# One over the deviation as a power on GpSimd, and a convolution's first products behind four PSUM copies

## Chip, cores, metric

One core of one Trainium2 chip. The metric is the device time of one execution in microseconds. All arithmetic is fp32. A program on one core shows no second die to compare with, so single runs are marked "unknown" in state; executions of the kernel before fall in two groups, near 3418 us and from 3435 to 3448 us.

## The reference, cut to what matters

A shifted-window transformer block on x of shape (16, 192, 56, 56), then a depthwise 3x3 convolution whose taps are computed from the mean of its input.

```
def _ln(x, g, b, eps=1e-05):
    mu = x.mean(-1, keepdims=True)
    var = ((x - mu) ** 2).mean(-1, keepdims=True)
    return (x - mu) / jnp.sqrt(var + eps) * g + b
# block: x1 = x + proj(attention(_ln(x)));  x2 = x1 + fc2(gelu(fc1(_ln(x1))))
# convolution: taps = f(mean(x2)), mask leaves 4 of 9 taps, one filter a channel
```

Each layer norm needs 1/sqrt(var + eps) for every pixel. The means are folded into the weights, so this factor is all that a norm applies.

## The kernel before

The 56 rows of an image are worked in four rounds, each on a strip of 7 rows in both halves. The first two rounds have no MLP (the two products fc1 and fc2) and two at the end have no attention; a short start and tail surround them. The statistics come from matmuls with a constant 1/192, already spread over groups of 32 partitions. `norm_devs` turns them into factors, for norm 1 of a later strip and norm 2 of an earlier one at once:

```
def norm_devs(keys):
    ...
    for s in sides:
        nc.scalar.activation(d[var[s]], stats[s][mean[s], :T], AF.Square)
    for s in sides:
        nc.vector.tensor_tensor(d[var[s]], stats[s][var[s], :T], d[var[s]], ALU.subtract)
    p = slice(0, 128) if len(sides) == 2 else var[sides[0]]
    nc.scalar.activation(d[p], d[p], AF.Sqrt, bias=eps_t[p])
    table(AF.Gelu)                        # a dummy that loads the table
    nc.vector.reciprocal(d[p], d[p])      # T = 392 columns
```

The main loop, with cuts:

```
for i in range(2, NS + 2):
    dev = norm_devs(keys)
    norm1_scale(i + 1, ...)               # VectorE
    norm_spread(keys, dev)                # 16 DMAs
    mlp_first(i - 2, ..., between)        # between: one convolution piece
    table(AF.Exp)
    attention_scores(i, ...)              # ends in 4 products "prob" on GpSimd
    table(AF.Sqrt)
    ys = [(*c, conv_begin(*c)) for c in conv_ready(2)]   # y = x * tap + bias, ScalarE
    mlp_out(i - 2, *mlp_second(i - 2, hid, turn))        # turn: PE transposes prob, ScalarE copies it
    yns[i - 1] = norm2_scale(...)         # GpSimd, needs the spread factors
    norm_squares(...)                     # GpSimd
    o = attention_values(i, prts)
    for c in ys: conv_rest(*c)            # 3 taps a piece, VectorE
    qs[i + 1] = attention_qk(i + 1)       # VectorE: kbd <- pk
    tail_of(i, o)                         # projection, then v
```

Each engine works its instructions in this order. `attention_turn` uses two PSUM buffers in turn, so the third turn needs the copy of the first.

Names of tiles in the profiles: `st` are the statistics, `dev` the factors and `dv` the factors spread over the partitions, `yn` and `win` the inputs scaled by them, `sq` the squares for the next statistics. `pk`, `pq`, `pe` and `pv` are the products for q, k and v in PSUM, `kbd` the keys copied out of it. `sc` are the scores, `e` their exponentials, `tot` one over their sum, `prob` the probabilities, `pt` the turned ones in PSUM and `prt` their copy. `po` and `o` are the values, `pp` the projection, `ph` and `pf` the two MLP products with `hid` between them. `y` is a piece of the convolution.

Of the kernel before, what the change touches and what calls it, by code (L numbers as in the profile page):

```python
# [8 lines left out]
F32 = mybir.dt.float32  # L9
AF = mybir.ActivationFunctionType  # L10
ALU = mybir.AluOpType
# [9 lines left out]
T = WS * IMG  # L21
# [8 lines left out]
EPS = 1e-5  # L30
# [6 lines left out]
def tile_swin_then_dynamic_conv(  # L37
# [31 lines left out]
    nc = tc.nc  # L69
# [4 lines left out]
    const = ctx.enter_context(tc.tile_pool(name="const", bufs=1))  # L74
# [7 lines left out]
    def bank(name, k):  # L82
        return psum.tile([128, 512], F32, tag=f"bank{k}", name=name)

    def banks(name, k):
        return psum.tile([128, 2, 512], F32, tag=f"banks{k}", name=name)

    def mm(dst, lhs, rhs, start, stop):
        nc.tensor.matmul(dst, lhs, rhs, start=start, stop=stop, skip_group_check=True)  # L89
# [81 lines left out]

    ident = const.tile([128, 128], F32, tag="ident", name="ident")
    eps_t = const.tile([128, 1], F32, tag="eps", name="eps_t")
    junk = const.tile([1, 1], F32, tag="junk", name="junk")

    sel = const.tile([128, 3, 32], F32, tag="sel", name="sel")
# [43 lines left out]
    def flat_of(i):  # L220
        v0, v1 = rows_of(i)
        return v0.rearrange("p h r c -> p h (r c)"), v1.rearrange("p r c -> p (r c)")

    sqs, stats = {}, {}

    def table(func):

        nc.scalar.activation(junk, eps_t[0:1], func)  # L228
# [28 lines left out]
    def norm_devs(keys):  # L257


        sides = sorted(keys)  # L260
        d = one.tile([128, T], F32, tag="dev", name=f"dev_{keys[sides[0]]}")
        mean = {s: slice(s * 64, s * 64 + 64) for s in sides}
        var = {s: slice(64 - s * 64, 128 - s * 64) for s in sides}
        for s in sides:
            nc.scalar.activation(d[var[s]], stats[s][mean[s], :T], AF.Square)
        for s in sides:
            nc.vector.tensor_tensor(d[var[s]], stats[s][var[s], :T], d[var[s]], ALU.subtract)
        p = slice(0, 128) if len(sides) == 2 else var[sides[0]]
        nc.scalar.activation(d[p], d[p], AF.Sqrt, bias=eps_t[p])  # L269
        table(AF.Gelu)  # L270
        nc.vector.reciprocal(d[p], d[p])  # L271
        stats.clear()
        return d

# [13 lines left out]
    def norm1_scale(i, dv, engine):  # L288

        v0, v1 = rows_of(i)  # L290
        b4 = dv.rearrange("p h (r c) -> p h r c", c=IMG)
        w0 = win0[:, :, :, 0:N].rearrange("p h w (r c) -> p h r w c", c=WS)
        w1_ = win1[:, :, 0:N].rearrange("p w (r c) -> p r w c", c=WS)
        cut = WS - SHIFT
        for ws, cs, at, n in (
            (slice(0, NWIN - 1), slice(0, WS), SHIFT, NWIN - 1),
            (slice(NWIN - 1, NWIN), slice(0, cut), IMG - cut, 1),
            (slice(NWIN - 1, NWIN), slice(cut, WS), 0, 1),
        ):
            m = n * (cs.stop - cs.start)  # L300

            def wide(v):
                return v[..., at : at + m]

            for h in range(2):
                engine.tensor_tensor(
                    w0[:, h, :, ws, cs],
                    wide(v0[:, h]).rearrange("p r (w c) -> p r w c", w=n),
                    wide(b4[:, h]).rearrange("p r (w c) -> p r w c", w=n),
                    ALU.mult,  # L310
                )
            for h in range(2):
                p = slice(h * 64, h * 64 + 64)
                engine.tensor_tensor(
                    w1_[p, :, ws, cs],
                    wide(v1[p]).rearrange("p r (w c) -> p r w c", w=n),
                    wide(b4[p, h]).rearrange("p r (w c) -> p r w c", w=n),
                    ALU.mult,
                )
# [268 lines left out]
    def mlp_second(i, hid, turn):  # L588
        pf1, pf = bank(f"pf1_{i}", 0), banks(f"pf_{i}", 2)
        for f in range(NFC):  # L590
            for a in range(2):
                mm(
                    pf1[a * 64 : a * 64 + 64, :T],
                    wf2[:, f, C0:DIM],
                    hid[:, f, a],
                    f == 0,
                    f == NFC - 1,
                )
        for f in range(NFC):
            for a in range(2):  # L600
                mm(pf[:, a, :T], wf2[:, f, 0:C0], hid[:, f, a], f == 0, f == NFC - 1)
            if f >= 2:
                turn(f - 2)
        return pf1, pf
# [3 lines left out]
    def mlp_out(i, pf1, pf):  # L608

        b, s = divmod(i, STEPS)  # L610
        if s == 0:
            sums[b] = small.tile([128, 2, STEPS], F32, tag="sums", name=f"sums_{b}")
        v0, v1 = flat_of(i)
        nc.vector.scalar_tensor_tensor(
            v1, pf1[:, :T], f2b[1], v1, ALU.add, ALU.add, accum_out=sums[b][:, 1, s : s + 1]
        )
        nc.vector.scalar_tensor_tensor(  # L617
            v0, pf[:, :, :T], f2b[0], v0, ALU.add, ALU.add, accum_out=sums[b][:, 0, s : s + 1]
        )
# [35 lines left out]
    def conv_begin(b, wt, n):  # L655

        kc, lo = (0, n * PR) if n < 4 else (1, (n - 4) * PR)
        y = work.tile([128, PR, IMG], F32, tag="y", name=f"y_{b}_{n}", bufs=3)
        nc.scalar.activation(  # L659
            y,  # L660
            images[b][kc][:, lo : lo + PR],
            AF.Identity,
            bias=cb[kc],
            scale=wt[:, kc, 1:2],
        )
        return y
# [36 lines left out]
    def has(i):  # L703
        return 0 <= i < NS

    def conv_ready(k):

        ready = []
        while k and convs and "wt" in convs[0]:
            c = convs[0]  # L710
            ready.append((c["b"], c["wt"], c["n"]))
            c["n"] += 1
            k -= 1
            if c["n"] == 6:
                convs.pop(0)
        return ready

    def stats_of(i):
        keys = {}
        if has(i + 2):  # L720
            keys[0] = f"1_{i + 2}"
            norm_stats(keys[0], i + 2, 0)
        if has(i - 1):
            keys[1] = f"2_{i - 1}"
            norm_stats(keys[1], i - 1, 1)
        return keys
# [9 lines left out]

    make_identity(nc, ident)
    nc.vector.memset(eps_t, EPS)
    nc.vector.memset(sel, 0.0)
    nc.vector.memset(sel[:, 0], 1.0 / DIM)  # L740
    nc.vector.memset(sel[0:64, 1], 1.0 / DIM)
# [49 lines left out]
    for c, at, lo, n, be, bias in (  # L791
# [5 lines left out]
        p = slice(at, at + n)  # L797
# [4 lines left out]
    for t in [kbd, vbd] + prob:  # L802
        nc.gpsimd.memset(t, 0.0)
    keys = stats_of(-1)
    dev = norm_devs(keys)
    norm1_scale(0, dvs.pop(0), nc.vector)
    dvs.update(norm_spread(keys, dev))
# [5 lines left out]
    for h in range(2):  # L813
        p = slice(h * 64, h * 64 + 64)
# [108 lines left out]
    for i in range(2, NS + 2):  # L923
        keys = stats_of(i)
        dev = norm_devs(keys) if keys else None
        if has(i + 1):
            norm1_scale(i + 1, dvs.pop(0), nc.vector)
        if keys:
            dvs.update(norm_spread(keys, dev))
        if (i + 3) % STEPS == 0 and (i + 3) // STEPS < B:  # L930
            b = (i + 3) // STEPS
            images[b] = load_x(b, nc.sync)

        def between():
            for b, wt, n in conv_ready(1):
                conv_rest(b, wt, n, conv_begin(b, wt, n))
            if convs and "pooled" in convs[-1]:
                convs[-1]["wt"] = taps(convs[-1]["b"], convs[-1].pop("pooled"))

        hid = one.tile([128, NFC, 2, T], F32, tag="hid", name=f"hid_{i - 2}")  # L940
        mlp_first(i - 2, yns.pop(i - 2), hid, between)
        if has(i):
            table(AF.Exp)
            attention_scores(i, *qs.pop(i))
        table(AF.Sqrt)
        ys = [(*c, conv_begin(*c)) for c in conv_ready(2)]
        prts = []

        def turn(wp):
            if has(i):  # L950
                prts.append(attention_turn(i, wp))

        mlp_out(i - 2, *mlp_second(i - 2, hid, turn))
        if 1 in keys:
            yns[i - 1] = norm2_scale(i - 1, dvs.pop(1))
        if has(i + 3):
            norm_squares(f"1_{i + 3}", i + 3, 0, nc.gpsimd)
        o = attention_values(i, prts) if has(i) else None
        for c in ys:
            conv_rest(*c)  # L960
        if has(i + 1):
            qs[i + 1] = attention_qk(i + 1)
        tail_of(i, o)
        if (i - 2) % STEPS == STEPS - 1:
            b = (i - 2) // STEPS
            convs.append({"b": b, "n": 0, "pooled": taps_pool(b)})
    c = convs.pop()
# [77 lines left out]
```

## Time and profile before

| | before |
|---|---|
| time, us | 3435.07 (3417.78 to 3435.66, 3 runs) |
| profiled span, us (an execution of 3416.78) | 3415.0 |
| TensorE busy | 95% |
| GpSimd busy | 22% |
| table loads on ScalarE | 193 of 1283 ns |
| wait of the transposes for ScalarE's copy | 86.4 us |
| reciprocal over 392 columns, VectorE | 2.60 us |

TensorE has no pause in a round but the one in front of the third turn. The lines are in the prediction. The starts of the first MLP product in the chain that ended last give the length of a round: 50.15, 50.14, 52.45 and 52.01 us in one image, the longer two being those with two convolution pieces behind the turns.

### The profile page before, as it was taken

How to read it: one execution, taken by the hardware profiler on the slowest of the kernel's cores; microseconds unless marked ns; L12 is line 12 of the kernel's file. 1: busy time of each engine (PE TensorE's matmuls, PEld its weight loads, DVE VectorE, ACT ScalarE, POOL GpSimd, SP SyncE). 2: the span in 40 equal slices, each digit the busy share in tenths (PEclk: the TensorE clock that was granted, in tenths of full speed). 3: DMA queues.
4: the chain of work that ended last, by engine and by line, in shares of the span. 5: the costliest groups of instructions: out<-in, count | busy, mean ns of one | idle time of the engine just before them, and what ended most of it. 6: DMA issues, size and time to landing. Idle time of an engine off the chain costs nothing.

```text
span 3415.0 us, 65067 instructions
## 1 busy us (share of the span) xinstructions
PE 3241.5 (95%) x26642; PEld 1917.0 (56%) x26642; DVE 2256.0 (66%) x4143; ACT 1755.0 (51%) x2863; POOL 745.6 (22%) x656
## 2 busy tenths in 40 slices
PE   4799999999999999999999999999999999999996
PEld 2455555555555555555555555555555555555553
DVE  5455676767667576676767667576676767667563
ACT  2355555555555555555555555555555555555552
POOL 4221221221221221221221221221221221221210
PEclk8799999999999999999999999999999999999998
DMA  3100111111011111111111011111111111011001
GB/s 94 19 20 23 46 39 48 34 53 34 25 48 44 43 34 40 42 39 48 34 53 34 25 48 46 41 34 39 44 39 48 34 53 34 25 48 46 12 29 44
DMA packets 79125, 135.40 MB, mean 40 GB/s; under 512 B 21766, under 2 KB 61692, under 8 KB 76908
## 3 DMA queue, kind: packets, MB, share of 16 engines
q1 hardware_dynamic: 77266, 128.54, 13.1%
q8 instruction: 210, 3.44, 0.4%
q0 software_dynamic: 1056, 1.92, 0.3%
q10 hardware_dynamic: 506, 0.79, 0.1%
q14 instruction: 87, 0.71, 0.1%
HBM read 41.25 MB, written 38.54 MB: 23 GB/s over the span
## 4 chain that ended last, share of the span: by engine, by line
PE 68%; DVE 20%; ACT 7%; issue 3%; DMA 1%; POOL 0%; SPq 0%; DVEq 0%; ACTq 0%; POOLq 0%
PE ph L89 24%; PE pv L89 7%; PE pp L89 7%; DVE top L459 6%; DVE e L453 5%; PE po L89 5%; PE st L89 5%; DVE e L460 5%; PE pk L89 4%; PE pq L89 4%; PE pe L89 4%; PE pf L89 3%; DVE tot L467 3%; PE pt L500 3%; ACT L228 2%
## 5 line engine op out<-in xcount | busy, mean ns | idle before, releaser
L469 POOL TENSOR_TENSOR prob<-e,tot 113x588 f32<-113x588 f32 x256 | 297.7, 1174 | 2483.4 <-PE pf L89 2177.1
L89 PE MATMUL ph<-yn,wf 128*128 128x392 f32 (+1 forms) x3072 | 818.6, 508 | 1.1 <-ACT hid L572 1.1
L89 PE MATMUL pf<-hid,wf 128*64 128x392 f32 (+1 forms) x3072 | 819.5, 498 | 0.0
L89 PEld LDWEIGHTS ph<-yn,wf 128*128 128x128 f32 (+1 forms) x3072 | 410.0, 188 | 401.2 <-ACT hid L572 84.8
L89 PEld LDWEIGHTS pf<-hid,wf 128*64 128x64 f32 (+1 forms) x3072 | 377.1, 164 | 310.8 <-issue 121.6
L572 ACT ACTIVATE hid<-ph,f1b 128x784 f32<-128x784 f32 x384 | 336.8, 913 | 243.2 <-PE ph L89 242.8
L360 DVE TENSOR_SCALAR kbd<-pk,qkb 32x784 f32<-32x784 f32 x256 | 263.8, 1030 | 254.8 <-PE pk L89 251.6
L463 ACT ACTIVATE e<-e 113x588 f32<-113x588 f32 x256 | 177.3, 693 | 466.5 <-DVE e L460 466.4
L674 DVE SCALAR_TENSOR_TENSOR y<-x,wt,y 128x770 f32<-128x770 f32 x288 | 322.9, 1131 | 22.7 <-ACT y L659 15.9
L453 DVE TENSOR_TENSOR e<-sc,bias_t 113x588 f32<-113x588 f32 x256 | 188.5, 737 | 190.0 <-PE sc L89 189.7
L500 PE MATMUL pt<-ident,prob 113*128 113x113 f32 x1536 | 195.3, 264 | 86.4 <-ACT prt L506 86.4
L89 PE MATMUL pv<-wqkv,win 64*128 64x192 f32 (+1 forms) x2048 | 273.1, 328 | 3.1 <-DVE kbd L360 3.1
L500 PEld LDWEIGHTS pt<-ident,prob 113*128 113x128 f32 x1536 | 168.7, 142 | 187.4 <-issue 131.2
L423 DVE COPY vbd<-pv 49x192 f32<-49x192 f32 x512 | 159.6, 350 | 172.2 <-PE pv L89 86.8
L89 PEld LDWEIGHTS pv<-wqkv,win 64*128 64x128 f32 (+1 forms) x2048 | 251.8, 188 | 35.3 <-issue 18.1
L89 PE MATMUL pp<-o,wp 128*128 128x392 f32 (+2 forms) x896 | 251.5, 521 | 1.6 <-ACT o L532 1.6
L228 ACT ACT_TABLE_LOAD x193 | 247.6, 1283 | 3.5
L617 DVE SCALAR_TENSOR_TENSOR x<-pf,cols,x 128x784 f32<-128x784 f32 x64 | 66.2, 1035 | 246.5 <-PE pf L89 246.5
L506 ACT COPY prt<-pt 128x678 f32<-128x678 f32 x256 | 176.9, 714 | 98.5 <-PE pt L500 98.5
L425 ACT COPY vbd<-pv 49x192 f32<-49x192 f32 x512 | 135.3, 312 | 151.8 <-DVE vbd L423 145.4
L271 DVE RECIPROCAL dev<-dev 128x392 f32<-128x392 f32 (+1 forms) x67 | 174.4, 2602 | 48.7 <-ACT dev L269 48.7
L460 DVE TENSOR_TENSOR e<-e,top 113x588 f32<-113x588 f32 x256 | 199.4, 779 | 8.7
(139 smaller groups left out, 4119.5 us busy)
## 6 DMA issues: line engine op xcount, KB each, us to landing
dv<-dev SPq DMA_DIRECT2D x1020, 49.0 KB
x<-in_x_dram SPq DMA_DIRECT2D x15, 1484.0 KB
out_dram<-y SPq DMA_DIRECT2D x48, 392.0 KB
out_dram<-y SPq DMA_DIRECT2D x48, 196.0 KB
x<-in_x_dram SPq DMA_DIRECT2D x16, 392.0 KB
x<-in_x_dram SPq DMA_DIRECT2D x15, 350.0 KB
out_dram<-y SPq DMA_DIRECT2D x16, 308.0 KB
out_dram<-y SPq DMA_DIRECT2D x16, 154.0 KB
```

The source lines that it names most:

```text
L89: nc.tensor.matmul(dst, lhs, rhs, start=start, stop=stop, skip_group_check=True)
L228: nc.scalar.activation(junk, eps_t[0:1], func)
L360: nc.vector.tensor_scalar(kbd[p, 0:2, :, h % 2, :], pk[p, :, :T].rearrange("p h (w t) -> p h w t", t=N), qkb[p, 1:2], None, ALU.add,)
L453: nc.vector.tensor_tensor(e, sc[:PW, :, : HEADS * N], rel, ALU.add)
L459: nc.vector.tensor_reduce(t, ehs[wp], AX.X, ALU.max)
L460: nc.vector.tensor_tensor(ehs[wp], ehs[wp], t.broadcast_to([PW, 2 * HEADS, N]), ALU.subtract)
L463: nc.scalar.activation(es[wp], es[wp], AF.Exp)
L469: nc.gpsimd.tensor_tensor(prob[wp][:PW, :, 0:N], ehs[wp], t.broadcast_to([PW, 2 * HEADS, N]), ALU.mult)
L500: nc.tensor.transpose(pt[:, a, g * PW : (g + 1) * PW], prob[wp][:PW, h : h + 2, :].rearrange("p h k -> p (h k)"), ident[:PW, :PW],)
L506: nc.scalar.copy(prt, pt[:, :, : 3 * PW])
L572: nc.scalar.activation(hid[:, f], phs[f][:, :, :T], AF.Gelu, bias=f1b[:, f : f + 1])
L674: nc.vector.scalar_tensor_tensor(dst, src, wt[:, kc, t : t + 1], dst, ALU.mult, ALU.add)
```

## The change

The intent is to take the root's table from ScalarE (three loads a round become two) and 2.6 us of reciprocal from VectorE, by putting one power on GpSimd, which is idle for over 30 us a round. The first products of the convolution then move behind the copies, so that nothing stands between the exponentials and the copies.

```diff
+    power = const.tile([128, 1], F32, tag="power", name="power")
...
-            nc.vector.tensor_tensor(d[var[s]], stats[s][var[s], :T], d[var[s]], ALU.subtract)
+            nc.vector.scalar_tensor_tensor(
+                d[var[s]], stats[s][var[s], :T], EPS, d[var[s]], ALU.add, ALU.subtract
+            )
         p = slice(0, 128) if len(sides) == 2 else var[sides[0]]
-        nc.scalar.activation(d[p], d[p], AF.Sqrt, bias=eps_t[p])
-        table(AF.Gelu)
-        nc.vector.reciprocal(d[p], d[p])
+        n = p.stop - p.start
+        nc.gpsimd.tensor_tensor(d[p], d[p], power[p].broadcast_to([n, T]), ALU.pow)
...
+    nc.vector.memset(power, -0.5)
...
-        table(AF.Sqrt)
-        ys = [(*c, conv_begin(*c)) for c in conv_ready(2)]
         prts = []
...
         mlp_out(i - 2, *mlp_second(i - 2, hid, turn))
+        table(AF.Gelu)
+        ys = [(*c, conv_begin(*c)) for c in conv_ready(2)]
```

## The prediction

> **What bounds the kernel now.** I read the page's first part, then the table of waits, then the timeline of one round of the main loop, engine by engine. One round handles one strip of seven rows in each image half: statistics, first MLP product, attention scores, second MLP product with the four transposes ("turns") of the probabilities between its steps, values, q/k, projection, v. There are 64 full rounds.
>
> ```profile
> PE 3241.5 (95%) x26642; PEld 1917.0 (56%) x26642; DVE 2256.0 (66%) x4143; ACT 1755.0 (51%) x2863; POOL 745.6 (22%) x656
> ```
>
> TensorE is busy 95% of 3415 us. It idles for only 174 us, and some 90 us of that lie in the start and the tail. So no change that leaves its products alone can win much over 2.5%. The table of waits names the one idle time that recurs every round:
>
> ```profile
> PE pt L500 <- ACT prt L506: 86.4, 64, 5.7
> ```
>
> That is 86.4 us in 64 waits, all in front of a transpose that waits for ScalarE to copy an earlier one out of PSUM (two buffers alternate, so the third turn needs the first one's copy). The timeline of a round with convolution work, and of one without, shows why the copy is late:
>
> ```profile
> 1064.66 0.69 ACT L463 ACTIVATE e<-e 113x588 f32<-113x588 f32 x1 [2.48 <-DVE e L460]
> 1065.37 1.28 ACT L228 ACT_TABLE_LOAD   x1
> 1066.66 0.20 ACT L228 ACTIVATE junk<-eps_t 1x1 f32<-1x1 f32 x1
> 1066.77 1.96 ACT L659 ACTIVATE y<-x,cols,wt 128x784 f32<-128x784 f32 x2
> 1068.64 1.31 ACT L506 COPY prt<-pt 128x678 f32<-128x678 f32 x2
> ...
> 1069.48 0.77 PE L500 MATMUL pt<-ident,prob 113*128 113x113 f32 x6 [2.22 <-ACT prt L506]
> ```
>
> ```profile
> 965.01 0.77 PE L500 MATMUL pt<-ident,prob 113*128 113x113 f32 x6 [0.35 <-ACT prt L506]
> ```
>
> Between the last exponential and the first copy stand the load of the root's table (1.4 us until the next instruction) and, in convolution rounds, two first products (1.96 us). TensorE then stands for 2.22 us, or for 0.35 us in the other rounds. My count of rounds: 15 images have their convolution behind a later image's rounds, each with two rounds that hold two such products, so 30 convolution rounds x 2.22 = 66.6 us. The other 32 ordinary rounds x 0.35 = 11.2 us. The first two rounds give the rest (2.56 and 5.66 us in their timeline). The sum is 86.0, against 86.4 in the table.
>
> VectorE's side of the same convolution round:
>
> ```profile
> 1071.62 1.03 DVE L617 SCALAR_TENSOR_TENSOR x<-pf,cols,x 128x784 f32<-128x784 f32 x1 [4.69 <-PE pf L89]
> 1072.58 0.08 DVE L617 DVE_READ_ACCUMULATOR x<-pf,cols,x 128x1 f32 x1
> 1072.58 3.22 DVE L674 SCALAR_TENSOR_TENSOR y<-x,wt,y 128x770 f32<-128x770 f32 x2
> 1075.83 0.19 DVE L683 COPY y<-cols 128x56 f32<-128x56 f32 x1
> 1076.06 4.06 DVE L674 SCALAR_TENSOR_TENSOR y<-x,wt,y 128x770 f32<-128x770 f32 x4
> 1080.16 4.17 DVE L360 TENSOR_SCALAR kbd<-pk,qkb 32x784 f32<-32x784 f32 x4
> ...
> 1085.10 1.14 PE L89 MATMUL pv<-wqkv,win 64*128 64x192 f32 x12
> ```
>
> From the MLP's addition to the end of the kbd eviction (1084.33) VectorE has no pause. The v product (pv) takes over the PSUM banks that kbd is read from, so it can't start before 1084.33. It starts at 1085.10, when TensorE gets there. **The slack is only 0.77 us.** This decides my prediction.
>
> **What the Trainium skill says.** "ScalarE: Activation LUTs", section "What ACT_TABLE_LOAD costs": about 1283 ns for the load plus about 1380 ns of drain. The trace agrees with the first (193 loads, 1283 ns each), but not with the second here: the next instruction starts 0.01 us after the load ends. So I count 1.4 us a load, not 2.66. "VectorE: DVE Perf Modes", section "First, the fixed hardware budget", has the reciprocal as an iterative divide with a repeat count of 8. The trace has 2.60 us for 392 columns, 6.4 cycles each at that page's 0.96 GHz. "GPSIMD Engine Reference", section 3.1, has no figure for a power. It gives some 2.6 cycles an element at 1.2 GHz for a two-input product and about three operations a cycle for longer bodies. The trace's 392-column square takes 0.84 us alone (1.56 us beside VectorE's convolution), which is 2.6 cycles. Section 8 of that page says that GpSimd contends with VectorE instructions with two SBUF inputs. The trace agrees: the two convolution taps that run beside GpSimd's last products take 1.61 us each, the next four 1.02 us.
>
> **The change, part by part.**
>
> Root and reciprocal go. ScalarE loses a root (0.62 us) and one of three table loads each round, VectorE 2.60 us. Both stand at the head of the round, behind which ScalarE waits for TensorE (0.83 us before the first GELU) and VectorE too (1.84 us before the first scores, 5.27 us without convolution). So these 2.6 us by themselves only lengthen waits and win nothing. What counts is that the load no longer precedes the copies.
>
> The power comes. The variance is ready at 1042.2 in this round and GpSimd is idle until 1059.4:
>
> ```profile
> 1059.40 1.17 POOL L469 TENSOR_TENSOR prob<-e,tot 113x588 f32<-113x588 f32 x1 [36.44 <-PE pf L89]
> ```
>
> So up to 17 us are free. The first turn starts at 1063.27 with its input done at 1060.57, so some 20 us cost little. Behind it, 16 DMAs spread the result, issued over 11.2 us with the half that this round uses first. GpSimd uses that at 1068, which leaves a power of up to some 16 us room too. If a power is 60 operations (my assumption) at the page's three a cycle, 392 columns take 6.5 us, an estimate. I take 8. That is free.
>
> The first products move behind the copies. The copies can then start at 1065.35, after the last exponential. The first is done at 1066.0, before TensorE reaches the third turn at 1067.26, and that turn's input from GpSimd is done at 1066.9. So the gap closes in every round. In ordinary rounds nothing else binds (VectorE waits 7.50 us for pk there): 32 x 0.35 = 11 us.
>
> In convolution rounds TensorE comes 2.2 us sooner, but VectorE doesn't. The fourth copy ends at about 1070.7. Then come the GELU load with its dummy (1.4) and the first product (1.03), so the first y is ready at 1073.15, against 1072.58 when VectorE begins its taps today. The taps and kbd take the same 11.75 us and end at 1084.9, and pv can start at 1084.95 rather than 1085.10: a gain of 0.15 us, not 2.2. In the other convolution round of an image, kbd waits 0.27 us for pk today, so the same sum gives 0.4 us. 15 x 0.15 + 15 x 0.4 = 8 us.
>
> The start: in the first two rounds the root and its loads precede the copies by 2.56 and 5.66 us of TensorE's idle time. I count 6 of these 8 us. The first scaling on VectorE no longer stands behind a reciprocal: 3 us. The tail has one GELU load less in front of a product: 1 us.
>
> The sum: 11 + 8 + 6 + 3 + 1 = 29 us, which makes 3417 into 3388. Two of the three runs of before took 3435, so a median may fall in either group. I take 3395.
>
> **The rivals.** (1) VectorE doesn't hold the convolution rounds, because the taps run faster when GpSimd's products lie beside the exponentials' end and not beside them. Then all 86 us come back: about 3330. Against it: six taps at 1.02 us still make 6.1 instead of 7.3 us, which frees 1.2 us a round at most, 30 x 1.2 = 36 us more, so about 3352; GpSimd's own times hardly move, so I expect little of that. (2) The power takes over 20 us. Then each us more holds up the probabilities, the turns and TensorE, 64 us for each us: a 30 us power makes about 4050. For it: no row here shows a power. Against it: 61 cycles a column are free, 23 times a product. (3) The ScalarE copies of the values (o) come behind load and products, to about 1075.0 in place of 1075.03, while TensorE is 2.2 us sooner and needs their bank for pe at about 1075.6. That is 0.5 us of slack; if it fails, convolution rounds may lose instead of gain: about 3405 to 3415.
>
> **Range and chances.** The sum gives about 1% and its parts are each bounded by a gap that I measured, so the middle is narrow: 3368 to 3425, the upper end for no gain in the slower group. Faster by over 2% needs over 68 of the 86 us, and so rival 1 in full: 8%. Slower by over 2% is rival 2: 12%. Within 2%: 80%.
>
> **What would show it.** The wait of pt for prt falls from 86.4 us to under 5. Table loads fall from 193 to some 130. Ordinary rounds fall from 50.15 to about 49.8 us. Convolution rounds stay above 51.4 us, with a new wait of pv for VectorE's kbd of some 2 us, 30 times, and a new wait of VectorE's taps for y. The power shows as a GpSimd row of 67 instructions under 17 us, and prob waits for tot as before. I am wrong if the power's row is over 20 us, or if convolution rounds fall to 50 us with no new wait.

## The result

The changed kernel takes **6433.6 us** (6432.49 to 6434.05, 4 runs), against 3426.68 us (4 runs) of the kernel before. The ratio is 1.877 (1.871 to 1.884). Ratios here are the mean time of one kernel's fast runs over that of the other's of the same rounds, so not quite the ratio of the medians.

The first part and the costliest groups of the page of the changed kernel (columns: line, engine, operation, tiles, shapes, count, then busy us and mean ns of one, then idle time before):

```profile
PE 3392.6 (53%) x26642; PEld 2003.7 (31%) x26642; DVE 2089.0 (32%) x4077; ACT 1614.2 (25%) x2654; POOL 4943.9 (77%) x723
...
L273 POOL TENSOR_TENSOR dev<-dev,power 128x392 f32<-128x392 f32 (+1 forms) x67 | 4223.2, 63033 | 1115.4 <-DVE dev L268 1092.1
```

GpSimd, at 22% before, is at 77%. One power takes 63.0 us, and there are 67. The table of waits of the changed kernel:

```profile
PE pt L502 <- POOL prob L471: 2667.9, 62, 43.6
```

No wait of the transposes for ScalarE's copy stands near the top any more. In its place they wait 43 us in each of 62 rounds for the probabilities. The timeline of GpSimd over one round shows the queue:

```profile
2012.06 63.05 POOL L273 TENSOR_TENSOR dev<-dev,power 128x392 f32<-128x392 f32 x1 [20.24 <-DVE dev L268]
2075.08 4.57 POOL L471 TENSOR_TENSOR prob<-e,tot 113x588 f32<-113x588 f32 x4
2082.56 1.84 POOL L327 TENSOR_TENSOR yn<-x,dv 128x784 f32<-128x784 f32 x1 [2.91 <-issue]
2084.36 2.10 POOL L330 TENSOR_TENSOR yn<-x,dv 64x392 f32<-64x392 f32 x2
2086.54 1.49 POOL L240 TENSOR_TENSOR sq<-x 128x784 f32<-128x784 f32 x1
2087.99 0.84 POOL L241 TENSOR_TENSOR sq<-x 128x392 f32<-128x392 f32 x1
2108.50 63.05 POOL L273 TENSOR_TENSOR dev<-dev,power 128x392 f32<-128x392 f32 x1 [19.66 <-DVE dev L268]
```

The four products that make the probabilities had their inputs by 2036.2. They run only when the power is done, at 2075, all four together. What follows is serial: turns, values, q/k, projection, statistics, and then the next variance, 33 us after the first product. A round lasts 63.05 + 33 = 96 us. Four power starts in a row lie 96.16, 94.94, 95.25 and 96.12 us apart.

TensorE also works more slowly just after such a pause. In this round its granted clock was 0.50 from 2076 to 2080 us, 0.90 to 2084 and 1.00 from 2085, and the first turn took 1.39 us where it takes 0.74 us in the kernel before. This is a small part: in all, TensorE's busy time grew from 3241.5 to 3392.6 us, by 151 of the 3007 us lost.

### The profile page after: what moved, and what is told of

The parts are those of the page before. It is cut to its first block, busy times and chain, and to the rows that moved or that the text cites. A ratio compares the mean times of both kernels' runs of the same rounds, so it can differ in the third digit from the quotient of the medians.

```text
span 6432.2 us, 65166 instructions
## 1 busy us (share of the span) xinstructions
PE 3392.6 (53%) x26642; PEld 2003.7 (31%) x26642; DVE 2089.0 (32%) x4077; ACT 1614.2 (25%) x2654; POOL 4943.9 (77%) x723
## 5 line engine op out<-in xcount | busy, mean ns | idle before, releaser
L273 POOL TENSOR_TENSOR dev<-dev,power 128x392 f32<-128x392 f32 (+1 forms) x67 | 4223.2, 63033 | 1115.4 <-DVE dev L268 1092.1
L502 PE MATMUL pt<-ident,prob 113*128 113x113 f32 x1536 | 254.5, 316 | 2668.4 <-POOL prob L471 2667.9
L502 PEld LDWEIGHTS pt<-ident,prob 113*128 113x128 f32 x1536 | 220.9, 177 | 2796.1 <-POOL prob L471 2706.8
L89 PE MATMUL pf<-hid,wf 128*64 128x392 f32 (+1 forms) x3072 | 904.1, 528 | 0.0
L89 PEld LDWEIGHTS pf<-hid,wf 128*64 128x64 f32 (+1 forms) x3072 | 413.4, 176 | 333.6 <-issue 162.2
L676 DVE SCALAR_TENSOR_TENSOR y<-x,wt,y 128x770 f32<-128x770 f32 x288 | 291.2, 1021 | 181.9 <-ACT y L661 175.1
L89 PE MATMUL st<-sq,sel 128*32 128x392 f32 x1024 | 189.0, 512 | 118.8 <-POOL sq L240 118.1
L327 POOL TENSOR_TENSOR yn<-x,dv 128x784 f32<-128x784 f32 x64 | 118.4, 1851 | 147.0 <-DMA dv<-dev 91.8
```

What stands on the lines that cost most here:

```text
L89: nc.tensor.matmul(dst, lhs, rhs, start=start, stop=stop, skip_group_check=True)
L273: nc.gpsimd.tensor_tensor(d[p], d[p], power[p].broadcast_to([n, T]), ALU.pow)
L502: nc.tensor.transpose(pt[:, a, g * PW : (g + 1) * PW], prob[wp][:PW, h : h + 2, :].rearrange("p h k -> p (h k)"), ident[:PW, :PW],)
L676: nc.vector.scalar_tensor_tensor(dst, src, wt[:, kc, t : t + 1], dst, ALU.mult, ALU.add)
```

## The experiments

Line numbers differ by a few between kernels. Each kernel gave a correct result.

### The power by itself

Twelve instructions behind the end of the kernel before, with nothing else to do:

```diff
+    nc.gpsimd.tensor_tensor(res, base, bc(half, al, T), ALU.pow)
+    nc.gpsimd.tensor_tensor(res, base, expo, ALU.pow)
+    nc.gpsimd.tensor_tensor(res, base, bc(unit, al, T), ALU.pow)
+    nc.gpsimd.tensor_tensor(res, flat1, bc(half, al, T), ALU.pow)
+    nc.gpsimd.tensor_tensor(res, base, bc(half, al, T), ALU.mult)
+    # then the power on 64, 16, 8, 1 partitions, and on 196, 49, 1 columns
```

> The kernel before, and after its end, on an otherwise idle chip, twelve instructions on GpSimd, each on a scratch tile: the power over 128 x 392 with the exponent -0.5 broadcast, with a full tile of exponents, with exponent 1, and with a base of all ones; a product of the same shape and operands; the power over 64, 16, 8 and 1 partitions x 392, and over 196, 49 and 1 columns. If the operation is a routine that is run for each column of 16 partitions whatever the values, all powers over 392 columns take 63 us, those of 196, 49 and 1 columns 31.8, 8.4 and 0.7 us (by the line through 63.05 and 16.2 us), and the product about 0.85 us. If each partition is worked one after the other, 8 partitions take half of 16 and 1 takes 4 us. If the broadcast of the exponent is the cost, the full tile of exponents is fast. If values decide, exponent 1 or base 1 is fast.

GpSimd's timeline of that run:

```profile
3440.05 62.89 POOL L987 TENSOR_TENSOR res<-base,half 128x392 f32<-128x392 f32 x1 [23.61 <-DVE unit L983]
3503.02 63.02 POOL L988 TENSOR_TENSOR res<-base,expo 128x392 f32<-128x392 f32 x1
3566.11 62.84 POOL L989 TENSOR_TENSOR res<-base,unit 128x392 f32<-128x392 f32 x1
3629.03 62.84 POOL L990 TENSOR_TENSOR res<-flat,half 128x392 f32<-128x392 f32 x1
3691.94 0.84 POOL L991 TENSOR_TENSOR res<-base,half 128x392 f32<-128x392 f32 x1
...
3881.57 62.83 POOL L995 TENSOR_TENSOR res<-base,half 1x392 f32<-1x392 f32 x1
3944.48 31.61 POOL L996 TENSOR_TENSOR res<-base,half 128x196 f32<-128x196 f32 x1
3976.16 8.15 POOL L997 TENSOR_TENSOR res<-base,half 128x49 f32<-128x49 f32 x1
3984.39 0.55 POOL L998 TENSOR_TENSOR res<-base,half 128x1 f32<-128x1 f32 x1
```

The cost follows the columns alone: (62.83 - 8.15) / (392 - 49) = 0.159 us a column. It is the same for 128 partitions and for one, for exponent -0.5 and 1, for a base of ones, and for a broadcast or a full tile of exponents. A product with the same operands takes 0.84 us, one seventy-fifth. The broadcast, the values and the neighbours are thereby ruled out. It is the operation. Why one column of it takes that long, no run here shows.

### The same kernel with a short power

```diff
-        nc.gpsimd.tensor_tensor(d[p], d[p], power[p].broadcast_to([n, T]), ALU.pow)
+        nc.gpsimd.tensor_tensor(d[p, :98], d[p, :98], power[p].broadcast_to([n, 98]), ALU.pow)
```

> The changed kernel with the power over only the first 98 of 392 columns (wrong result on purpose; the others keep the variance). If the power's time goes with its columns, 63.05 x 98/392 = 15.8 us, which is under the 17 us that GpSimd has free: then the kernel takes what I predicted for a free power, 3380 to 3400, ratio near 0.99, and prob waits for tot again. If the power has a large fixed part or slows the other engines in some other way, the row is over 20 us and the kernel well over 3500.

Measured: 3403.86 us, ratio 0.995 (0.992 to 0.998). The comparison called the result correct all the same: probably because the variance of this input is near 1, so that its root hardly shows within the tolerance (not tested). The power takes 16.2 us, and GpSimd is then idle until it gets its input:

```profile
1009.18 16.21 POOL L273 TENSOR_TENSOR dev<-dev,power 128x98 f32<-128x98 f32 x1 [11.14 <-DVE dev L268]
1026.71 1.17 POOL L471 TENSOR_TENSOR prob<-e,tot 113x588 f32<-113x588 f32 x1 [1.32 <-PE pf L89]
```

Rounds take 49.61, 49.60, 51.49 and 51.30 us, as in "both moved" below, to 0.02 us. That version keeps root and reciprocal, so taking them off the head of the round won nothing there, as predicted. So in the main loop a power of 16.2 us really is free, and GpSimd has 1.3 us to spare in this round. The start isn't free: the first full MLP product begins at 202.1 us against 172.7 us there, and TensorE waits for GpSimd's squares in three places:

```profile
PE st L89 <- POOL sq L240: 25.4, 3, 12.9
```

That is why 3404 came and not the 3380 to 3400 I expected.

```diff
+        nc.gpsimd.tensor_tensor(d[p, :196], d[p, :196], power[p].broadcast_to([n, 196]), ALU.pow)
```

> The changed kernel with the power over 196 of 392 columns (wrong result on purpose). By the two lengths measured the row takes 31.8 us. Loop theory: a round lasts as long as the power plus some 31 to 33 us from the first prob to the next variance, here 63 to 65 us, in place of 49.6 to 51.4: about 62 x 13 = 800 us more than the kernel with 98 columns and some 50 more at the start, so 4150 to 4350. If a power over 17 us costs in another way (each instruction behind it late by the full power), a round is 50 + 31.8 and the kernel about 5300.

Measured: 4366.08 us (one run), a little over the range. The row is 31.8 us, the rounds 64.13, 64.49, 65.39 and 65.35 us. The mean of these four rounds less the power is 33.0 us. With the whole power it is 32.6 us (the four rounds of one image in the result above), so the loop theory holds.

### The power without the move

```diff
+        ys = [(*c, conv_begin(*c)) for c in conv_ready(2)]
         prts = []
...
         table(AF.Gelu)
-        ys = [(*c, conv_begin(*c)) for c in conv_ready(2)]
```

> The changed kernel with the first products back in their old place; only the power in place of root and reciprocal. Theory A: the power's row is 63 us again and the round is 63 us and some 33 us from the first prob to the next variance, so 6400 to 6470, as the changed kernel. The move of the products is lost in TensorE's wait for prob either way. If the moved products had a share in the loss, it is faster by over 50 us.

Measured: 6430.71 us (one run), 3 us under the changed kernel, power 63.05 us. The move of the products has no part in the loss.

### The probabilities out of GpSimd's queue

```diff
-            nc.gpsimd.tensor_tensor(
+            nc.vector.tensor_tensor(
                 prob[wp][:PW, :, 0:N], ehs[wp], t.broadcast_to([PW, 2 * HEADS, N]), ALU.mult
             )
```

> The changed kernel with its power of 63 us on GpSimd, but the four products that make the probabilities on VectorE, so that they no longer stand behind the power in GpSimd's queue. Theory A (the queue is the cost): TensorE no longer waits for prob; what is left is GpSimd's own turn of power, the wait for the spread (some 8 us), scaling 4 and squares 2.3, near 78 us a round: 5200 to 5500. Rival: it is the need for the power's result itself that holds the round; then a round stays at 95 us and the kernel at 6400.

Measured: 5680.23 us (one run). TensorE's wait for the probabilities falls from 2667.9 to 60.9 us. Power starts lie 82 us apart, every fourth about 89 us, where I had said 78. So both have a share: the queue in front of the probabilities costs some 12 us a round, and the rest stays because GpSimd alone has 63 us of power, a wait for the spread and its scaling, and the squares stand behind these. The waits show the latter:

```profile
PE st L89 <- POOL sq L240: 1331.1, 48, 60.2
...
PE st L89 <- DMA x<-in_x_dram: 480.7, 25, 34.5
POOL yn L327 <- DMA dv<-dev: 424.2, 64, 7.0
```

The second of these lines belongs to the longer fourth rounds. There the next image's load stands in SyncE's queue behind the 16 DMAs of the spread, and these wait for the power. In one such round the spread was issued from 2032.56 us, the load from 2042.66 us, and the statistics that needed x started at 2049.91 us.

The range of 5200 to 5500 was missed; the direction was right. Moving the queue's victims does not save a 63 us instruction.

### The move without the power

The root and the reciprocal stay; the root's load and both products go behind the copies:

```diff
-        table(AF.Sqrt)
-        ys = [(*c, conv_begin(*c)) for c in conv_ready(2)]
...
         mlp_out(i - 2, *mlp_second(i - 2, hid, turn))
+        table(AF.Sqrt)
+        ys = [(*c, conv_begin(*c)) for c in conv_ready(2)]
```

> The kernel before with its root and reciprocal; only the load of the root's table and the two first products move behind the four copies of the turned tiles. The order on ScalarE, VectorE and TensorE is then that of the changed kernel, without the power. Theory A (the power's length is the whole loss, and the rest of my sum was right): the wait of pt for prt falls from 86.4 us to under 5, ordinary rounds from 50.15 to 49.8 us, convolution rounds stay near 51.6 us because VectorE's taps then wait for y and pv for kbd (some 2 us, 30 times). In the first two rounds the root's load still stands ahead of the copies, so 8 us of that stay. In all 3417 goes to about 3398, ratio 0.993 to 0.997. Theory B (VectorE does not bind convolution rounds): all of the 66 us of those rounds come back, ratio about 0.977. Theory C (the reordering costs too): ratio over 1.

Measured: 3375.8 us, ratio 0.987 (0.985 to 0.989). That is more than expected. Two of TensorE's waits in that kernel:

```profile
PE pv L89 <- DVE kbd L360: 40.3, 30, 3.1
...
PE pt L500 <- ACT prt L506: 8.0, 2, 5.4
```

The second has fallen from 86.4 us to 8.0 us (the first two rounds, whose loads I left alone). The first is new but for one wait of 3.1 us that the kernel before has too: 29 waits of some 1.3 us, 37 us. So nearly half of the recovered 78 us is given back by VectorE. VectorE's timeline of one such round, with TensorE's line that follows it, shows why:

```profile
1058.79 0.08 DVE L617 DVE_READ_ACCUMULATOR x<-pf,cols,x 128x1 f32 x1
1061.62 2.82 DVE L674 SCALAR_TENSOR_TENSOR y<-x,wt,y 128x770 f32<-128x770 f32 x2 [2.74 <-ACT y L659]
1064.47 0.19 DVE L683 COPY y<-cols 128x56 f32<-128x56 f32 x1
1064.69 4.06 DVE L674 SCALAR_TENSOR_TENSOR y<-x,wt,y 128x770 f32<-128x770 f32 x4
1068.67 4.16 DVE L360 TENSOR_SCALAR kbd<-pk,qkb 32x784 f32<-32x784 f32 x4
...
1072.89 4.37 PE L89 MATMUL pv<-wqkv,win 64*128 64x192 f32 x32 [1.41 <-DVE kbd L360]
```

VectorE stands 2.74 us for y, which now comes behind copies and load. Taps and kbd take 11.2 us from there, and pv waits 1.41 us for their end.

Each half of the move alone, on one chip. Only the load moved:

```diff
-        table(AF.Sqrt)
         ys = [(*c, conv_begin(*c)) for c in conv_ready(2)]
...
+        table(AF.Sqrt)
```

> The kernel before with only the load of the root's table moved behind the copies; the two first products stay ahead of them. Theory A (in convolution rounds VectorE's taps must start with the MLP's addition): the copies come 1.4 us sooner in every round and y is ready before the addition ends, so that VectorE's chain moves with TensorE's. Ordinary rounds 49.6 us as with both moved (0.55 less than before), convolution rounds 1.4 us shorter rather than the 0.85 us of both moved: 32 x 0.55 + 30 x 1.4 = 60 us, 3357, ratio 0.982 to 0.984, faster than both moved. If what counts is how soon the copies come, it is slower than both moved: the gap of 0.8 us before the third turn stays in 30 rounds, and the ratio is 0.988 or more.

Measured: 3361.27 us, ratio 0.981 (0.978 to 0.985), rounds 49.60, 49.61, 51.06, 50.88 us. The wait of the turns has not gone, but pv waits for kbd only once, 3.1 us, as in the kernel before:

```profile
PE pt L500 <- ACT prt L506: 29.5, 32, 4.9
```

Only the products moved:

```diff
         table(AF.Sqrt)
-        ys = [(*c, conv_begin(*c)) for c in conv_ready(2)]
...
+        ys = [(*c, conv_begin(*c)) for c in conv_ready(2)]
```

> The kernel before with only the two first products moved behind the copies; the root's load stays ahead of them. Ordinary rounds stay at 50.15 us with their wait of 0.35 us. Convolution rounds: the copies come 1.96 us sooner, y is ready about 0.5 us sooner than in the kernel before because no load stands between copies and products; with the slack of 0.77 us of pv the round is 0.8 to 1.3 us shorter: 25 to 40 us, ratio 0.988 to 0.993. If the products ahead of the copies were harmless, ratio 1.0.

Measured: 3392.44 us, ratio 0.990 (0.987 to 0.994), rounds 50.14, 50.15, 51.51, 51.30 us.

The load alone moved beats both moved by some 14 us. Those two runs were on different chips, but the rounds say the same: 51.06 and 50.88 us against 51.50 and 51.30 us. Once the load is out of the way, putting the products behind the copies costs: in a convolution round TensorE gains 0.7 us in front of the turn ((29.5 - 8.0) / 30) and loses 1.3 us in front of pv.

### Versions that beat both kernels

The first products in the pauses that ScalarE has between copies, the first behind the second copy and the second behind the third:

```diff
-        table(AF.Sqrt)
-        ys = [(*c, conv_begin(*c)) for c in conv_ready(2)]
+        ready = conv_ready(2)
+        ys = []
...
         def turn(wp):
             if has(i):
                 prts.append(attention_turn(i, wp))
+            if wp in (1, 2) and ready:
+                c = ready.pop(0)
+                ys.append((*c, conv_begin(*c)))
         mlp_out(...)
+        table(AF.Sqrt)
```

> As behind_both, but the two first products stand each behind a turn: the first behind the second copy, the second behind the third copy, where ScalarE waits for TensorE for 0.34 and 1.19 us today. If VectorE's waiting for y is what keeps the convolution rounds long (theory A), y is then ready when VectorE ends the MLP's addition, and pv starts when TensorE gets there: convolution rounds near 49.9 us, total about 3417 - 66 - 11 = 3340, ratio 0.977 to 0.98. If it is VectorE's work itself and not its wait, or the PSUM banks, the ratio stays where behind_both is.

Measured: 3350.38 us, ratio 0.980 (0.977 to 0.982): faster, though not clearly by 2%. VectorE's waits for y are back at what they were before (16.4 us, against 98.4 us with both moved), and pv waits less for kbd:

```profile
PE pv L89 <- DVE kbd L360: 18.0, 29, 3.1
```

I had expected no such wait; the convolution rounds take 50.74 and 50.51 us. What is left is VectorE's own work there. Taps and kbd take 13.3 us in the round that I looked at (1054.57 to 1067.83 us), against 11.2 us with both moved, and the small copy into y takes 1.36 us there and 0.19 us above. More of this work now lies beside GpSimd's products, which end at 1059.89 us. That these are the reason is inferred from the overlap.

So the last version spreads that work: `conv_ready(1)` in place of `conv_ready(2)`, the product behind the second turn only. Six pieces fall on an image's rounds as 1, 2, 2, 1 and not 2, 3, 1, 0, and the others go into a place where VectorE waits for scores.

> The kernel before with root and reciprocal, the root's load behind the copies, and at most one convolution piece behind the turns in any round (its first product behind the second turn's copy), the others between the halves of the first MLP product, where VectorE waits for scores anyway: six pieces over four rounds as 1, 2, 2, 1 in place of 2, 3, 1, 0. Theory A (VectorE's work between the MLP's addition and kbd binds the convolution rounds): the wait of pv for kbd, 40 us with both products behind the copies and 18 us threaded, goes to 3 or less; rounds near 49.6 us, total 3330 to 3340, ratio 0.974 to 0.977. If something else lengthens convolution rounds, the ratio stays near 0.980.

Measured: **3326.72 us**, ratio 0.971 (0.968 to 0.975), faster than both and a little below the 3330 to 3340 expected. Rounds take 49.61, 49.60, 50.05 and 49.61 us, and no wait of pv for kbd stands among TensorE's seven longest waits:

```profile
PE pt L500 <- ACT prt L506: 8.2, 2, 5.9
```

## Why the prediction was wrong, step by step

**The step that failed** is the sentence "If a power is 60 operations (my assumption) at the page's three a cycle, 392 columns take 6.5 us, an estimate. I take 8. That is free." The power takes 63.05 us, eight times what I took. At 1.2 GHz ("GPSIMD Engine Reference", section 1) 0.159 us is some 191 cycles a column, an estimate, where I had 20. The count of 60 operations had no source in the page or the trace. It decided the result, and I gave its failure (rival 2) 12%.

**Rival 2's room was nearly right.** It said that some 20 us cost little and that each us more costs 64 us. (It counted 64 full rounds; there are 62, as its own sum of the gaps has it, and five powers outside them.) The run with 16.2 us shows no cost in the rounds. A round of the power plus 33.0 us passes 50.5 us at a power of 17.5 us, an estimate from the two shortened runs; 20 us was not run. Between 196 columns and all, each us cost (6433.6 - 4366.08) / (63.05 - 31.82) = 66 us. For the whole power the sum runs: a mean round of 95.62 us less 50.50 us (with the short power), each from the four rounds of one image, is 45.1 us, times 62 rounds, 2797 us. The five powers outside these rounds are each 63.05 - 16.21 us longer, 234 us. Together 3031 us. The two medians differ by 3030 us. What rival 2 lacked is the start and tail, where nothing hides a power: in the changed kernel the first full MLP product begins at 384.9 us and not at 172.7 us.

**The gap in front of the turns** closed, as predicted: with both moved and the root kept, 86.4 us became 8.0 us, all of it in the first two rounds. In the changed kernel the loads fell from 193 to 124 (I said 130).

**The ordinary rounds** were to gain 0.35 us and gained 0.54 us (50.15 to 49.61). So that term is 17 us, not 11. The other 0.2 us lay in the same place. From the start of the four products pf behind the second turn to the third turn, the kernel before takes 1.85 us (248.58 to 250.43) and the one with only the load moved 1.33 us (249.32 to 250.65). That is 0.52 us shorter, of which the view counts only 0.35 us as idle.

**The convolution rounds** were to be held by VectorE, with a new wait of pv for kbd. That is the mechanism that the runs show. The term was mis-sized: I had a gain of 0.15 us for the round shown and 0.4 us for the other, and it was 0.7 us (52.01 to 51.30) and 0.95 us (52.45 to 51.50), 25 us and not 8. Taps and kbd took 11.2 us and not 11.75 us, mostly because they begin later against GpSimd's products (inferred from the overlap): the first two taps took 2.82 us and not 3.22 us. My rival 1 named this shift, and I had put it aside as little. The wait is 1.3 us, 29 times, and not 2.

**The start** was to gain 9 us. With a power of only 16.2 us it lost 29 us already. GpSimd has its squares queued behind the power there, which I did not check.

**Rival 3** (the copies of o too late for pe) did not happen: in the convolution round with both moved, pe starts without a wait.

## What to carry to other kernels

Moving an operation to an idle engine needs the duration of that very operation on that engine; if no row and no page has it, measure it alone first, for one instruction behind the end of the kernel costs one run. An in-order engine that is idle most of the time is no free room for an instruction longer than its pause, because short ones that others wait for stand behind it. When a gap on the busiest engine is closed, look at once for the engine that has the least slack behind it: here half of the gain came back only when the taps were spread over the rounds.

## What the Trainium skill lacked or had wrong

- "GPSIMD Engine Reference", section 3, has no figure for the power. The runs show 0.159 us a column (an estimate of 191 cycles at the 1.2 GHz of its section 1) and 0.55 us for one column. For 392 columns it was 62.8 us with any of the partition counts and values tried, against 0.84 us for a product. The rule in section 3.1 of about three operations a cycle is no guide to such an operation unless the count is known.
- "GPSIMD Engine Reference", section 4.1, has GpSimd about 2x slower than VectorE for a two-input add, product or maximum, and no row for a power. The product that makes the probabilities took 1.17 us on GpSimd and 0.77 us on VectorE, 1.5x. A root and a reciprocal as one power took 62.8 us on GpSimd, against 0.62 us on ScalarE and 2.60 us on VectorE.
- "ScalarE: Activation LUTs", section "What ACT_TABLE_LOAD costs": the load is 1283 ns, as stated. The drain of about 1380 ns did not show: in the round shown the load started 0.02 us after the last exponential ended, the next instruction 0.01 us after the load ended, and moving one load out of the way shortened a convolution round by 1.39 us and 1.13 us.
